# Wider mixer scores, paused scans and another queue for weights in a four-layer convolution stack

## The chip, the cores and the metric

The kernel runs on one core of one Trainium2 chip. The core has five engines that work beside each other, each on a queue of its own: TensorE (PE in the profile) multiplies matrices, VectorE (DVE) and ScalarE (ACT) work elementwise, GpSimd (POOL) too, and SyncE (SP) issues transfers. The metric is the device time of one execution, in microseconds (us); lower is better. The time before is the median of three runs.

## The reference

The input has 8 images of 256 channels and 32 x 32 places (1024 tokens), in float32. Four layers follow one another, each of the form `x = x + layer(group_norm(x))`, where the group norm has 32 groups and no weights:

- Layer 0 is attention over the 1024 tokens with 8 heads of 64, cosine similarities times 10, and an output projection.
- Layers 1 and 2 are 3 x 3 convolutions, 256 to 256 channels.
- Layer 3 is a long block. It has four Mamba branches (a selective scan over the 1024 tokens, 128 channels x 16 states each), gates and short depthwise convolutions, a second attention with 8 heads of 32 (called the mixer attention here) beside a local depthwise convolution, a joint projection, a layer norm with GELU, a norm over the image, a 3 x 3 depthwise convolution, a layer norm and a last projection.

Cut to what matters here:

```python
x = x + L0(gn(x))            # attention: 8 heads of 64
x = x + conv3x3_a(gn(x))
x = x + conv3x3_b(gn(x))
h = gn(x)
xm  = 4 x selective_scan(layernorm(h))
xm2 = mix(h, xm)
att = softmax(q @ k.T / sqrt(32)) @ v        # 8 heads of 32, from xm2
out = concat(depthwise3(xm2), att) @ fc      # then gelu(layernorm), image norm,
x = x + proj(layernorm(depthwise3x3(out)))   # depthwise 3x3, layernorm, proj
```

## The kernel before, in words

Everything stays in float32. A channel tile is 128 partitions x 1024 tokens, two of them to an image; every matmul has 512 columns where it can.

The work of an image falls into three streams, which belong to different images at one time. `front_attention` and `front_convs` are layers 0 to 2 of image b+1. `scan_layers` is the Mamba part of image b. `back_layers`, `back_out` and `back_end` are the rest of image b-1. The loop at the end of `preact_stack` runs over the images; its `dense()` strings together the first and third stream, and `interleave(dense(), scan_layers(imgs[b]), PACE[b])` weaves the scans between them.

The order is written out by hand. Each generator yields a cost, roughly the PE time of what it has just emitted. `interleave` adds up these costs and emits one scan step whenever the sum has passed another `pace` (1.37 in the middle images, 0.9 in the first, 0.74 in the last), so many steps at once if the cost was large. A scan step is a quarter of a scan unit: the two decays on ACT (`da`), the drive and the weighing on POOL (L956 and L981), the two scans on DVE (`hs`), and after every second unit eight matmuls `y<-hs,sel`. `Paced` adds an order between scan instructions and the last dense instruction of the same engine, so that a scan step doesn't come ahead of the dense work that it was written after. A planner then places the instructions on the engines in order of priority; `urgent()` raises the small operations of a norm outside the scans. All compute calls of `tensor`, `vector` and `scalar` have the line L102 in the profile, the line of the helper; they are told apart by their tiles.

Names that the steps below use:

- `chunk` (L156) loads a block of weights into one of five buffers (`wsp`), by a transfer that SyncE issues. A load waits until PE has used the block five loads earlier. 48 such loads are made for an image.
- `attention` is used by both attentions. A unit is one key block of 128 for two heads: two score matmuls into `big`, an exponential `p<-big` on ACT, and two value matmuls `acc<-p,v`. 64 units make an image. Each float32 matmul shows as two PE instructions in the profile.
- The two score matmuls of a unit lie on different rows of the array. In layer 0 a head has 64 rows (`big<-q,k`, 64*128). In the mixer attention a head has 32 rows (`big<-qk,qk`, 32*128), and the two heads i and i+1 of a pair lie on neighbouring strips.
- `mixer_attention` makes v, then the four projections `qk` (two of q, two of k), then runs the four pairs. `back_layers` computes the local convolution (`local`) before it, and starts the next image's group norm (`begin`) at step 58 of it.
- `group_norm` needs a chain: statistics of the finished tile on DVE, a small matmul with `gmat`, a few operations, a second one, then an inverse root by ten or so small DVE operations (`inverse_root`), then two scalings on ACT that write `im<-xt,shift,rs`, the padded images that the convolution reads.
- `front_convs` yields 4 times for the output projection (13.76 of cost), once after the first group norm, 36 times (1.73 each) for the first convolution, once after the second group norm, and 36 times again.
- `back_end` (the end of the image before: layer norm, image norm, sixteen depthwise operations `dw<-xo,vec,dw` on DVE, layer norm, projection) is dropped into `front_convs` by `amid`, at places that are sums of cost:

```python
ENDS = [74, 77, 88, 99, 114]
[0, 13.7, 20] + [23 + 2.7 * k for k in range(16)] + ENDS
```

At the end a flag is computed from the sums of the softmax. Where it is set, a second version of the layers runs; with these inputs it doesn't.

Of the kernel before, what the change touches and what calls it, by code (L numbers as in the profile page):

```python
# [11 lines left out]
F32 = mybir.dt.float32  # L12
I32 = mybir.dt.int32
AF = mybir.ActivationFunctionType
ALU = mybir.AluOpType
# [18 lines left out]
def preact_stack(ctx: ExitStack, tc: tile.TileContext, I, out, cols):  # L34
# [29 lines left out]
    def work(name):  # L64
        return tp.tile([P, TP], F32, tag="t", name=name)
# [4 lines left out]
    def big_tile():  # L70
        return ps_big.tile([P, N], F32, tag="big", name="big")
# [68 lines left out]
    def col(name, i=0, rows=slice(0, P)):  # L140
        at = cols[name] + i
        return vec[rows, at : at + 1]
# [7 lines left out]
    def chunk(name, i):  # L150

        src = fc_w if name == "fcw" else I[name]
        k, n = src.shape[2:]
        t = wsp.tile([P, HALF], F32, tag="w", name="w")
        t = t[:, 0 : k * n].rearrange("p (k n) -> p k n", n=n)
        nc.sync.dma_start(out=t, in_=src[i])  # L156
        return t

    minw = resident("minw")
# [59 lines left out]
    fc_w = wdp.tile([2, P, 4, P], F32, tag="fc_w", name="fc_w")  # L219
    half_d = wp.tile([P, NB], F32, name="half_d")  # L220
    vector.tensor_scalar_mul(half_d, vec[:, cols["mD"] : cols["mD"] + NB], 0.5)
    half_qb = wp.tile([P, 2], F32, name="half_qb")
    vector.tensor_scalar_mul(
        half_qb, vec[:, cols["qpwb"] : cols["qpwb"] + 2], 0.5
# [846 lines left out]
    def mixer_attention(x2, img, exact=False):  # L1071


        v = vp.tile([P, NKT, 8, 64], F32, tag="v", name="v3")
        vector.memset(v[:, :, :, 32:64], 1.0)
        wv = chunk("ainv", 0)
        for kt in range(0, NKT, 4):
            ps = big_tile()
            for i in range(4):
                for c in range(2):  # L1080
                    tensor.matmul(
                        ps[:, i * C : (i + 1) * C],
                        inner(x2[c])[:, (kt + i) * P : (kt + i + 1) * P],
                        wv[:, c],
                        start=c == 0,
                        stop=c == 1,
                    )
            vector.tensor_copy(
                v[:, kt : kt + 4, :, 0:32],
                ps.rearrange("p (k a b) -> p k a b", k=4, b=32),  # L1090
            )
            yield 3.8

        qk = {}
        for t in (0, 2, 1, 3):
            qk[t] = work("qk3")
            w = chunk("ainqk", t)
            ps = big_tile()
            for h in range(2):
                for c in range(2):  # L1100
                    tensor.matmul(
                        ps[:, HALVES[h]],
                        w[:, c],
                        inner(x2[c])[:, HALVES[h]],
                        start=c == 0,
                        stop=c == 1,
                    )
            scale = 32.0**-0.5 if t < 2 else 1.0
            vector.tensor_scalar(
                qk[t][:, 0:N], ps, col("ain_b", t), scale, ALU.add, ALU.mult  # L1110
            )
            yield 3.4

        o = img["o3"] = [work("o3_0"), work("o3_1")]

        def head(i):
            t, rows = i // 4, slice((i % 4) * 32, (i % 4) * 32 + 32)

            def take(half, acc):

                vector.tensor_copy(o[t][rows, half], acc)

            return {
                "q": qk[t][rows, 0:N],
                "k": qk[2 + t][rows, 0:N],
                "v": lambda kt: v[:, kt, i, 0:32],
                "rows": rows,
                "take": take,
            }

        if exact:
            attention_exact(head(i) for i in range(8))
            return

        sums = {}

        def pair(i):
            t = i // 4
            rows = [slice((j % 4) * 32, (j % 4) * 32 + 32) for j in (i, i + 1)]

            def v_of(j):
                return lambda kt: v[:, kt, j]

            def take(h, acc, _):
                if t not in sums:
                    sums[t] = dp.tile([4, N], F32, tag="sums4", name="sums")
                both = half_work("both")
                scalar.copy(both, acc)
                for e in range(2):
                    j, at = (i + e) % 4, e * 64  # L1150
                    nc.sync.dma_start(
                        out=o[t][rows[e], HALVES[h]], in_=both[at : at + 32]
                    )
# [4 lines left out]
                if i % 4 == 2 and h == 1:  # L1158
                    ot = o[t][:, 0:N]

                    return invert(
                        sums[t], 4, 32, lambda r: vector.tensor_mul(ot, ot, r)
                    )

            return {
                "q": [qk[t][r, 0:N] for r in rows],
                "k": [qk[2 + t][r, 0:N] for r in rows],
                "v": [v_of(i), v_of(i + 1)],
                "take": take,
            }  # L1170

        yield from attention([lambda i=i: pair(i) for i in range(0, 8, 2)], False)

    def back_layers(img, exact=False, begin=None):

# [80 lines left out]
        yield from project("fpw", fd, evac_x2)  # L1256


        local = [work("local0"), work("local1")]
        for t in range(2):  # L1260
            depthwise3(local[t][:, 0:N], x2[t], "lc_w", "lc_b", t)
        for n, cost in enumerate(mixer_attention(x2, img, exact)):
            yield cost
            if n == 58 and begin is not None:
                next(begin)
        img["mix"] = xt, local

    def merge_weights():
# [142 lines left out]
    def drain(*streams):  # L1411
        for s in streams:
            for _ in s:
                pass
# [17 lines left out]
    def amid(stream, other, places):  # L1432
# [7 lines left out]
            spent += cost  # L1440
        yield from other

    def slow(stream):

        for cost in stream:
            yield SLOW * cost

    SLOW = 0.35

    ENDS = [74, 77, 88, 99, 114]  # L1450
    PACE = [0.9] + [1.37] * (batch - 2) + [0.74]
    imgs = [{} for _ in range(batch)]
    drain(
# [3 lines left out]
    for b in range(batch):  # L1457

        def dense():
            last = imgs[b - 1] if b > 0 else None  # L1460
            front = None
            if b + 1 < batch:
                front = front_attention(image_of(b + 1), imgs[b + 1])
            if last is None:
                yield from front
                yield from front_convs(imgs[b + 1])
                return
            for n, cost in enumerate(back_layers(last, begin=front)):
                yield cost
                if n == 2 and front is not None:  # L1470
                    next(front)
            if front is None:
                yield from back_out(last)
                yield from back_end(last, out[b - 1])
                return
            yield from islice(front, 4)
            yield next(front)
            yield from back_out(last)
            yield from slow(front)
            yield from amid(  # L1480
                front_convs(imgs[b + 1]),
                back_end(last, out[b - 1]),
                [0, 13.7, 20] + [23 + 2.7 * k for k in range(16)] + ENDS,
            )

        interleave(dense(), scan_layers(imgs[b]), PACE[b])
# [132 lines left out]
```

## Time and profile before

| what | value |
|---|---|
| time | 6742.33 us, median of 3 (6730.57 to 6764.84) |
| span of the profiled execution | 6722.0 us, 52091 instructions |
| PE busy | 5656.0 us (84%) |
| DVE busy | 3779.4 us (56%) |
| ACT busy | 2682.4 us (40%) |
| POOL busy | 2683.7 us (40%) |
| mean granted TensorE clock | 0.868 |
| chain that ended last, by engine | PE 59%, DVE 20%, DMA 6%, issue 6%, ACT 6% |
| SyncE's weight loads (L156) waiting for PE | 1424.4 us in 209 waits, the longest 90.1 us |

How to read it: the first 1018 us hold the fronts of the first two images and the first image's scans. Then come six stretches of about 792 us, in each of which one image ends, one is scanned and one begins; a seventh of 627 us without a front, and a last one of 308 us in which the last image ends alone. A stretch starts with the first matmul of `back_layers`. [...] at 0.5 a matmul takes twice as long, and PE is as busy as at 1.0. "PE busy" must therefore be read together with the clock.

### The profile page before, as it was taken

The page shows a single profiled execution, that of the slowest core. Times are in us where ns is not written, and L with a number is a line of the kernel's source. Part 1 is how long each engine was busy: PE and PEld are TensorE (multiplying, and loading weights), DVE is VectorE, ACT ScalarE, POOL GpSimd, SP SyncE. Part 2 cuts the span into 40 slices and gives each one's busy share as a digit, 9 for nine tenths or more (in the row PEclk, how much of TensorE's full clock was granted, in tenths as well). Part 3 has the DMA queues.
Part 4 walks back from the last instruction along what each step waited for, and adds up shares of the span by engine and source line. Part 5 has one row for each costly group of instructions (what it writes and reads, how often), then busy time and mean ns, then how long its engine had stood idle before and what let it go on. Part 6 is the DMA issues. An engine that isn't in the chain of part 4 may idle for free.

```text
span 6722.0 us, 52091 instructions
## 1 busy us (share of the span) xinstructions
PE 5656.0 (84%) x17318; PEld 1896.2 (28%) x17318; DVE 3779.4 (56%) x4611; ACT 2682.4 (40%) x3225; POOL 2683.7 (40%) x1297
## 2 busy tenths in 40 slices
PE   8886688996989969998789979899799997968586
PEld 2331133222422234222332223222242223411132
DVE  4247855567446674466645674556743667444522
ACT  3223424553245432554236442455324543234332
POOL 0006662634246250643516343362514535166500
PEclk9987898998989979898888989799897997967697
DMA  1022332322224132321223222231213312232200
GB/s 48 26 59 73 86 84 72 93 66 63 72 74 109 42 82 67 91 76 55 68 70 95 76 63 73 64 109 51 78 53 86 95 48 76 73 82 69 83 21 29
DMA packets 216695, 470.80 MB, mean 70 GB/s; under 512 B 60120, under 2 KB 101720, under 8 KB 214368
## 3 DMA queue, kind: packets, MB, share of 16 engines
q1 hardware_dynamic: 216416, 467.38, 25.1%
q8 instruction: 139, 2.28, 0.1%
q14 instruction: 140, 1.15, 0.1%
HBM read 394.31 MB, written 64.49 MB: 68 GB/s over the span
## 4 chain that ended last, share of the span: by engine, by line
PE 59%; DVE 20%; DMA 6%; issue 6%; ACT 6%; POOL 2%; SPq 1%; ACTq 0%; POOLq 0%; DVEq 0%
PE big L102 36%; PE acc L102 14%; PE da L102 5%; DVE hs L102 5%; PE y L102 3%; DVE dw L102 3%; DVE p L102 2%; DVE u L102 2%; DMA dt<-dt_m 1%; DMA dt_m<-dt 1%; POOL hs L956 1%; ACT da L102 1%; ACT p L102 1%; DVE dt L102 1%; DVE t L102 1%
## 5 line engine op out<-in xcount | busy, mean ns | idle before, releaser
L956 POOL TENSOR_TENSOR hs<-du,bc 128x1024 f32<-128x1024 f32 x512 | 1292.3, 2540 | 1613.4 <-DMA dt<-dt_m 1421.9
L981 POOL TENSOR_TENSOR hs<-hs,bc 128x1024 f32<-128x1024 f32 x512 | 1279.6, 2500 | 959.3 <-DVE hs L102 772.1
L102 ACT ACTIVATE p<-big 128x1024 f32<-128x1024 f32 x1024 | 1039.8, 1021 | 941.3 <-PE big L102 921.5
L102 PE MATMUL acc<-p,v 128*64 128x512 f32 x4096 | 1239.8, 672 | 17.1 <-ACT o L102 15.4
L102 PE MATMUL big<-im,w 128*128 128x512 f32 x2304 | 1085.6, 625 | 88.7 <-ACT im L102 78.1
L102 ACT ACTIVATE da<-dt,a_neg 128x512 f32<-128x512 f32 x1024 | 697.1, 688 | 945.7 <-DVE hs L102 787.1
L102 DVE TENSOR_TENSOR_SCAN hs<-da,hs 128x512 f32<-128x512 f32 x512 | 610.2, 1213 | 581.2 <-ACT da L102 367.6
L102 DVE TENSOR_TENSOR_SCAN hs<-da,carry,hs 128x512 f32<-128x512 f32 x512 | 632.1, 1269 | 374.8 <-POOL hs L956 208.1
L102 DVE TENSOR_TENSOR p<-p 128x1024 f32<-128x1024 f32 x448 | 672.0, 1500 | 283.2 <-ACT p L102 169.1
L102 PE MATMUL big<-qk,qk 32*128 32x512 f32 x2048 | 712.3, 736 | 74.6 <-ACT p L102 72.0
L102 PE MATMUL big<-q,k 64*128 64x512 f32 x2048 | 626.7, 663 | 70.4 <-ACT big L102 30.7
L102 PEld LDWEIGHTS big<-im,w 128*128 128x128 f32 x2304 | 443.5, 198 | 725.9 <-issue 613.6
L980 POOL COPY carry<-hs 128x2 f32<-128x2 f32 x256 | 122.3, 478 | 1093.6 <-DVE hs L102 1078.1
L102 PEld LDWEIGHTS acc<-p,v 128*64 128x64 f32 x4096 | 223.3, 143 | 909.3 <-issue 802.4
L102 PE MATMUL y<-hs,sel 128*32 128x512 f32 x2048 | 361.9, 683 | 79.3 <-POOL hs L981 79.3
L102 PEld LDWEIGHTS big<-qk,qk 32*128 32x128 f32 x2048 | 184.0, 207 | 595.1 <-issue 281.4
L102 PE MATMUL da<-xn,w_minw 64*128 64x512 f32 x256 | 171.3, 756 | 213.0 <-DVE hs L102 197.2
L102 PEld LDWEIGHTS big<-q,k 64*128 64x128 f32 x2048 | 172.0, 192 | 498.9 <-issue 264.1
L102 DVE SCALAR_TENSOR_TENSOR dw<-xo,vec,dw 128x961 f32<-128x961 f32 (+1 forms) x128 | 221.8, 1783 | 29.1 <-ACT dw L102 29.1
L102 PE MATMUL big<-xn,w 128*128 128x512 f32 x512 | 230.0, 600 | 1.2 <-DVE v L102 1.2
L102 PE MATMUL big<-o,w 128*128 128x512 f32 x384 | 179.6, 618 | 10.0 <-DVE o L102 10.0
L102 DVE SCALAR_TENSOR_TENSOR xt<-big,vec,xt 128x1024 f32<-128x1024 f32 x48 | 61.5, 1280 | 196.5 <-PE big L102 196.5
(208 smaller groups left out, 4942.2 us busy)
## 6 DMA issues: line engine op xcount, KB each, us to landing
bc<-bc SPq DMA_DIRECT2D x1024, 128.0 KB
dt<-dt_m SPq DMA_DIRECT2D x512, 128.0 KB
du<-du_m SPq DMA_DIRECT2D x512, 128.0 KB
w<-in_wc SPq DMA_DIRECT2D x192, 192.0 KB
rs<-inv SPq DMA_DIRECT2D x64, 256.0 KB
dt_m<-dt SPq DMA_DIRECT2D x64, 256.0 KB
du_m<-a SPq DMA_DIRECT2D x64, 256.0 KB
xt<-in_x SPq DMA_DIRECT2D x8, 1024.0 KB
```

Source lines behind the costliest of these rows:

```text
L102: made = issue(*args, **kwargs)
L956: nc.gpsimd.tensor_mul(u["hs"], u["du"], both_groups(u["bc"][:, 0]))
L980: nc.gpsimd.tensor_copy(carry[:, u["q"], g : g + 2], hs[:, :, HALF - 1])
L981: nc.gpsimd.tensor_mul(hs, hs, both_groups(u["bc"][:, 1]))
```

## The change

Five edits are made at once.

1. **64-row mixer scores.** The k of a projection tile (four heads of 32 rows) is used as it is, 64 rows at a time. q is written twice, once with the rows of the odd heads set to zero (by DVE) and once with those of the even heads (by ACT), through the column pair `alt` of scales. A score matmul then has 64 rows, in which only one head counts. A pair is now heads i and i+2, and the pairs are 0, 1, 4 and 5.
2. **The second q and k inside the mixer.** `q_and_k(1)` is made when its first pair is asked for, eight units ahead of its use, instead of before the mixer.
3. **The local convolution inside the mixer**, at its steps 34 and 40, instead of before it.
4. **Pauses of the scans (`lull`) and other places for the image's end.** In the steps 0 to 3 and 35 to 40 of `front_convs` the cost is held back, so that no scan steps are emitted ahead of the two group norms; it is paid with the step after. `back_end` begins at 14.7 of cost, behind the first group norm, instead of 0, and its last parts stand later.
5. **Weights on ScalarE's queue.** `chunk` issues its transfers from ACT instead of SyncE.

```diff
-        nc.sync.dma_start(out=t, in_=src[i])
+        nc.scalar.dma_start(out=t, in_=src[i])
...
+    alt = wp.tile([P, 2], F32, name="alt")
+    nc.gpsimd.memset(alt, 0.0)
+    for g in range(4):
+        nc.gpsimd.memset(alt[g * 32 : g * 32 + 32, g % 2 : g % 2 + 1], 32.0**-0.5)
+    alt_b = wp.tile([P, 2, 2], F32, name="alt_b")
+    for t in range(2):
+        vector.tensor_scalar_mul(alt_b[:, t], alt, col("ain_b", t))
...
-        for t in (0, 2, 1, 3):
-            qk[t] = work("qk3")
...
+        def q_and_k(t):
+            for at in (t, 2 + t):
+                w = chunk("ainqk", at)
...
+                if at == t:
+                    q = [work("qk3")[:, 0:N] for _ in range(2)]
+                    vector.tensor_scalar(
+                        q[0], ps, col("ain_b", t), alt[:, 0:1], ALU.add, ALU.mult
                     )
-            scale = 32.0**-0.5 if t < 2 else 1.0
-            vector.tensor_scalar(
-                qk[t][:, 0:N], ps, col("ain_b", t), scale, ALU.add, ALU.mult
-            )
-            yield 3.4
+                    scalar.activation(
+                        q[1], ps, AF.Identity, bias=alt_b[:, t, 1:2], scale=alt[:, 1:2]
+                    )
+                else:
+                    k = work("qk3")[:, 0:N]
+                    vector.tensor_scalar_add(k, ps, col("ain_b", at))
+                yield 3.4
+            qk[t] = q, k
+
+        yield from q_and_k(0)
...
+            if t not in qk:
+                drain(q_and_k(t))
+            q, k = qk[t][0][i % 2], qk[t][1]
...
-                "q": [qk[t][r, 0:N] for r in rows],
-                "k": [qk[2 + t][r, 0:N] for r in rows],
-                "v": [v_of(i), v_of(i + 1)],
+                "q": [q[e * 64 : e * 64 + 64] for e in range(2)],
+                "k": [k[e * 64 : e * 64 + 64] for e in range(2)],
+                "v": [v_of(i), v_of(i + 2)],
...
-        yield from attention([lambda i=i: pair(i) for i in range(0, 8, 2)], False)
+        yield from attention([lambda i=i: pair(i) for i in (0, 1, 4, 5)], False)
...
-        local = [work("local0"), work("local1")]
-        for t in range(2):
+        local = []
+
+        def add_local():
+            t = len(local)
+            local.append(work("local"))
             depthwise3(local[t][:, 0:N], x2[t], "lc_w", "lc_b", t)
+
         for n, cost in enumerate(mixer_attention(x2, img, exact)):
             yield cost
-            if n == 58 and begin is not None:
+            if n in (34, 40):
+                add_local()
+            if n == 56 and begin is not None:
                 next(begin)
...
+    def lull(stream, spans):
+
+        owed = 0.0
+        for n, cost in enumerate(stream):
+            if any(a <= n < b for a, b in spans):
+                owed += cost
+                yield 0.0
+            else:
+                yield cost + owed
+                owed = 0.0
...
-    ENDS = [74, 77, 88, 99, 114]
+    LULLS = (0, 4), (35, 41)
+
+
+    ENDS = [14.7, 18, 24] + [27 + 2.5 * k for k in range(16)] + [79, 84, 92, 99, 112]
...
-                front_convs(imgs[b + 1]),
+                lull(front_convs(imgs[b + 1]), LULLS),
                 back_end(last, out[b - 1]),
-                [0, 13.7, 20] + [23 + 2.7 * k for k in range(16)] + ENDS,
+                ENDS,
```

More of the change, by code (lines that the diff above doesn't have):

```diff
@@ L1094, in mixer_attention @@
         qk = {}
-        for t in (0, 2, 1, 3):
-            qk[t] = work("qk3")
[L1097 to L1106, printed above, removed]
-                    )
-            scale = 32.0**-0.5 if t < 2 else 1.0
-            vector.tensor_scalar(
-                qk[t][:, 0:N], ps, col("ain_b", t), scale, ALU.add, ALU.mult
-            )
-            yield 3.4
+        def q_and_k(t):
+            for at in (t, 2 + t):
+                w = chunk("ainqk", at)
+                ps = big_tile()
+                for h in range(2):
+                    for c in range(2):
+                        tensor.matmul(
+                            ps[:, HALVES[h]],
+                            w[:, c],
+                            inner(x2[c])[:, HALVES[h]],
+                            start=c == 0,
+                            stop=c == 1,
+                        )
[3 more added lines that the diff above has]
+                        q[0], ps, col("ain_b", t), alt[:, 0:1], ALU.add, ALU.mult
+                    )
+                    scalar.activation(
+                        q[1], ps, AF.Identity, bias=alt_b[:, t, 1:2], scale=alt[:, 1:2]
+                    )
+                else:
[4 more added lines that the diff above has]
+        yield from q_and_k(0)
         o = img["o3"] = [work("o3_0"), work("o3_1")]
@@ L1121, in take @@
                 vector.tensor_copy(o[t][rows, half], acc)
+            if t not in qk:
+                drain(q_and_k(t))
             return {
-                "q": qk[t][rows, 0:N],
-                "k": qk[2 + t][rows, 0:N],
+                "q": qk[t][0][i % 2][rows],
+                "k": qk[t][1][rows],
                 "v": lambda kt: v[:, kt, i, 0:32],
@@ L1138, in pair @@
             t = i // 4
-            rows = [slice((j % 4) * 32, (j % 4) * 32 + 32) for j in (i, i + 1)]
+            if t not in qk:
+                drain(q_and_k(t))
+            q, k = qk[t][0][i % 2], qk[t][1]
             def v_of(j):
@@ L1149, in take @@
                 for e in range(2):
-                    j, at = (i + e) % 4, e * 64
+                    j, at = i % 4 + 2 * e, e * 64
                     nc.sync.dma_start(
-                        out=o[t][rows[e], HALVES[h]], in_=both[at : at + 32]
+                        out=o[t][j * 32 : j * 32 + 32, HALVES[h]],
+                        in_=both[at : at + 32],
                     )
@@ L1157, in take @@
                     )
-                if i % 4 == 2 and h == 1:
+                if i % 4 == 1 and h == 1:
                     ot = o[t][:, 0:N]
@@ L1263, in back_layers @@
             yield cost
-            if n == 58 and begin is not None:
+            if n in (34, 40):
+                add_local()
+            if n == 56 and begin is not None:
                 next(begin)
+        while len(local) < 2:
+            add_local()
         img["mix"] = xt, local
```

## The prediction

> **What bounds the kernel now.** I read the page's 40 slices first, then the span cut at the stage boundaries of one image, then the granted clock inside the worst stage, and last the time line around the waits.
>
> ```profile
> PE   8886688996989969998789979899799997968586
> PEclk9987898998989979898888989799897997967697
> ```
>
> PE (TensorE) is busy 84% of the span and no other engine over 56%, but the second line is not flat: the granted clock averages 0.868. Lost clock is lost time on the engine that bounds. One typical image (2601.8 to 3397.7 us, 796 us; its neighbours take 791 to 792) in four stages: up to the mixer's attention, mixer attention, the next image's attention, its convolutions; then the mixer attention of the seventh such stretch, beside the last image's scans:
>
> ```profile
> core 0: us, PE busy (x) PEld busy (x) DVE busy (x) ACT busy (x) POOL busy (x), PEclk, DMA share, GB/s
> 2601.80:2679.30 77.50, 69.43 (x203) 34.94 (x201) 58.72 (x96) 33.63 (x35) 0.00 (x0) 0.91 0.19 62
> 2679.30:2893.90 214.60, 190.70 (x623) 43.32 (x622) 98.67 (x96) 116.83 (x143) 133.80 (x69) 0.83 0.34 90
> 2893.90:3129.20 235.30, 216.72 (x754) 62.81 (x752) 163.35 (x183) 117.60 (x145) 82.83 (x38) 0.96 0.24 65
> 3129.20:3397.70 268.50, 214.34 (x593) 91.82 (x592) 151.66 (x198) 66.76 (x82) 118.37 (x54) 0.86 0.25 71
> 5867.00:6247.30 380.30, 292.13 (x747) 58.59 (x748) 176.72 (x152) 161.21 (x204) 244.85 (x124) 0.69 0.33 84
> ```
>
> The clock records hold two values, 1.0 and 0.5, so a stage's half-clock time is 2 x (1 - PEclk) x length: 73 us in the mixer attention, 19 us in the next image's attention, 75 us in the convolutions. In the mixer PE works through most of it; in the convolutions about half of it is PE standing still. Why the mixer stays slow, in four stretches (same columns):
>
> ```profile
> 2685.60:2716.20 30.60, 27.89 (x58) 5.79 (x60) 4.67 (x4) 11.91 (x14) 12.96 (x8) 0.50 0.35 85
> 3115.70:3119.10 3.40, 3.40 (x10) 0.80 (x8) 0.32 (x1) 1.60 (x2) 0.00 (x0) 0.50 0.00 1
> 3119.10:3125.00 5.90, 5.90 (x24) 1.20 (x20) 5.69 (x6) 2.90 (x3) 0.00 (x0) 1.00 0.01 1
> 6480.00:6600.00 120.00, 118.98 (x462) 28.70 (x464) 1.71 (x4) 64.76 (x67) 0.00 (x0) 1.00 0.05 13
> ```
>
> The 32-row mixer attention runs 30 us at half clock with PE busy 91%. The 64-row attention, after a cold start, is at full clock after one full stretch of 3.4 us. The last line is the mixer of the last image, which began at full clock and kept it: 32 rows don't cause the drop, they fail to end it. I cut the whole trace into the 3.41 us steps on which the clock changes and took half-clock steps in which matmuls stream at least 80% of the time: with mixer scores in them 105 of 108 are followed by another half-clock step, with the first attention's scores 3 of 21. The drops themselves follow waits:
>
> ```profile
> 2684.72 1.28 ACT L102 ACT_TABLE_LOAD   x1 [21.44 <-DMA dt<-dt_m]
> 2688.31 2.08 PE L102 MATMUL big<-qk,qk 32*128 32x512 f32 x4 [6.47 <-ACT p L102]
> 3159.04 0.39 PE L102 MATMUL acc<-mv,gmat 128*128 128x4 f32 x2 [3.64 <-DVE mv L102]
> 3162.82 0.58 PE L102 MATMUL acc<-d,gmat 128*128 128x2 f32 x2 [3.39 <-DVE d L102]
> 3182.12 2.92 PE L102 MATMUL big<-im,w 128*128 128x512 f32 x3 [7.62 <-ACT im L102]
> 3243.64 2.07 PE L102 MATMUL da<-xn,w_minw 64*128 64x512 f32 x2 [22.66 <-DVE hs L102]
> 245.43 4.78 PE L102 MATMUL big<-im,w 128*128 128x512 f32 x7 [3.96 <-ACT im L102]
> ```
>
> The first two: ACT holds a scan's exponential for a transfer, and the mixer's exponentials stand behind it. The next three: the first group norm takes from 3154 (last output-projection matmul) to 3182, 28 us; the last line is the same place in the first image, without scans, where it took from 236.3 to 245.4, 9.1 us. Then PE waits 22.66 us for DVE in the first convolution.
>
> [...]
>
> **The change part by part**, per typical image unless said.
>
> *64-row scores.* Four matmuls a unit remain and take 1.06 us at full clock with either row count (start to start of scores and values at 2767.87 and 2991.23), so nothing is saved directly. What changes is the exit from half clock: every score pair now fills all 128 rows. PE records overlap 59 of the 73 us; half of it, 29.5 us, is lost now. The gaps (6.5, 5.9, 2.6, 4.2 us) mostly stay, because PE still waits in order for scan work. I take three or four cold stretches of 7 us, as in the next stage (19 us in two), 17 us of PE work in all, 8.5 lost: 21 us saved. In the sixth of these stretches (5058.6 to 5283.1, clock 0.77, so 103 us cold, 94 with PE) it is 35. In the seventh (last row of the stage table) 236 us are cold, 176 with PE: 88 at most; POOL, busy 245 of 380, becomes the next limit and its waits cool PE again: 75. The last image's is at full clock already: 0. Half the rows of q are zero. If the gate counts values instead of occupied rows, the whole part is worth 0; no run shows it. I take occupied rows.
>
> *Second q and k inside the mixer.* 7 us of PE work (half of the 13.9 us for four projections) moves from before the mixer into it: 0. Two more ACT operations of 1.24 us: hidden, ACT is busy 117 of 215 there.
>
> *Local convolution into the mixer.* Four DVE operations of 1.28 us and two of ACT leave a stage in which PE idles only 8 of 77.5 us: 0.
>
> *Lulls, and the image end behind the first norm.* In the new order no scan stands between the statistics and the shift on DVE, at either group norm. At the first, PE still has 32 small layer-norm matmuls (about 7 us) ahead of the convolution, so not 9 but 13 us: 28 - 13 = 15, I take 14. At the second, 17 us from 3299 to 3316, these matmuls (6.96 us in one row) now stand behind the convolution's first ones: 10 us, 6 saved. The scans held back (13.76 cost, 10 steps, 2.5 scan units of 2 x 1.24 us on DVE, then 7 steps) come at once afterwards. The first convolution takes 117 us (3182 to 3299) with DVE busy 87 and PE 89; in the new order the wait of 22.66 us falls later and with 62 instead of 30 of the convolution's 72 matmuls ahead of it, but DVE's sum grows to about 90. I take 6 us saved. The second convolution gets the layer-norm matmuls and late scans: 5 us lost. Sum 21.
>
> *Weights on ACT.* The wait for fc_w (6.03 us at 2925) goes, since its load now stands in the mixer: 5.5. 48 issues of 0.33 us make 16 us of ACT's sequencer: hidden. Each can also hold ACT until PE frees a buffer; behind it are p and da, for which PE and the scans wait. In the new order each load stands near the matmul that frees its buffer, so I take 0; the other end is below. Two more table loads, 2.6 us: hidden, ACT is busy 67 of 268 there.
>
> Sum: 21 + 21 + 5.5 = 47.5 us in each of five images, 35 + 26.5 = 61.5 in the sixth, 75 in the seventh; first 1018 us and last 308 us: 0. 237.5 + 61.5 + 75 = 374, and 6742 - 374 = **6368, say 6370 us**.
>
> **The rivals.**
> - *The gate counts values, or waits cool PE as often as before.* For it: half of q is zero. Against: the layout of occupied rows alone separates 105 of 108 from 3 of 21. The 215 us of the mixer are missing (5 x 21 + 35 + 75): 6585.
> - *DVE takes back what the lulls give.* For it: DVE is busy 52 of 64 us in the first convolution's first part already. Then the 21 us are missing six times: 6370 + 126 = 6496.
> - *Weight loads hold ACT.* For it: SyncE's 1424 us in 209 waits, 178 us an image. If a third of them delayed PE, 59 us an image would be lost in eight images: 6370 + 472 = 6842, slower.
>
> **How the numbers follow.** Forecast 0.62, gate 0.12, DVE 0.16, ACT slower 0.10. The lower end: POOL no limit in the seventh stretch, one cold stretch of 7 us less and 15 us more from the first convolution in each image, some 150 us: 6220. The upper end takes in the first two rivals and the missing fc_w gain: 6640. Faster 0.86, same 0.04, slower 0.10.
>
> **What would show it.** Right: clock over 0.92 in mixer stages and the seventh under 320 us; 12 to 15 us to the first convolution; no wait on fc_w. Wrong: half-clock stretches of 20 us in the mixer, a PE wait over 20 us for DVE in the first convolution, or ACT idle before p with the releaser a weight buffer.

## The result, and the profile after

The changed kernel takes 6547.26 us (median of 4 runs, 6539.40 to 6553.38) against 6736.45 us of the kernel before on the same chip (4 runs): ratio 0.9719, 95% interval 0.9674 to 0.9763. It is faster by 189 us; 374 had been forecast (6370 us). The time lies in the range, and half of the gain is missing.

The page of the changed kernel, PE and its clock in 40 slices:

```profile
PE   8886788998889979899889988899889998867596
PEclk9997889999999989999999999899889998978697
```

The mean granted clock rose from 0.868 to 0.900; the dips beside the mixers are mostly gone, the drop near the end is not. The clock records hold 1.0 and 0.5 alone and, but for one in each run, last multiples of 3.41 us; at 0.5 a record `big<-im,w` begins 0.85 us after the one before it, at 1.0 0.43 us (medians of either kernel). The stages of the changed kernel that answer to those shown of before (up to the mixer's attention, mixer attention, next image's attention, convolutions with the image end, and the seventh mixer attention). The columns are busy time of each engine with its number of instructions, the granted clock, DMA share and rate:

```profile
core 0: us, PE busy (x) PEld busy (x) DVE busy (x) ACT busy (x) POOL busy (x), PEclk, DMA share, GB/s
2556.50:2628.60 72.10, 62.55 (x187) 31.82 (x185) 52.99 (x91) 33.55 (x35) 0.00 (x0) 0.91 0.18 59
2628.60:2828.30 199.70, 176.67 (x628) 44.05 (x630) 103.42 (x99) 117.57 (x143) 129.91 (x67) 0.91 0.37 97
2828.30:3053.00 224.70, 216.07 (x754) 62.16 (x754) 163.57 (x178) 117.96 (x144) 87.74 (x38) 0.98 0.25 68
3053.00:3321.60 268.60, 224.04 (x601) 90.92 (x602) 164.35 (x205) 71.13 (x86) 121.19 (x56) 0.90 0.26 73
5691.80:6055.10 363.30, 259.86 (x753) 57.18 (x754) 178.83 (x153) 165.98 (x207) 234.80 (x119) 0.79 0.34 87
```

Against the rows of before: 5 us less up to the mixer's attention, 15 less in it (clock 0.83 to 0.91), 11 less in the next image's attention, and **nothing in the convolutions**, 268.5 before and 268.6 after, though the lulls and the late image end were made for that stage. The seventh mixer attention gives 17 us where 75 were forecast. The first stretch, to the first matmul of `back_layers`, grew from 1018.5 to 1028.1 us.

PE's time line at the first group norm of the same image (start, duration, engine, line, operation, number, and in brackets the wait before it and what ended it):

```profile
3075.95 5.40 PE L102 MATMUL big<-o,w 128*128 128x512 f32 x8 [1.99 <-DVE o L102]
3084.28 0.59 PE L102 MATMUL acc<-mv,gmat 128*128 128x4 f32 x2 [2.94 <-DVE mv L102]
3085.52 0.59 PE L102 MATMUL acc<-d,gmat 128*128 128x2 f32 x2 [0.65 <-DVE d L102]
3086.04 1.93 PE L102 MATMUL y<-hs,sel 128*32 128x512 f32 x8
3087.90 6.99 PE L102 MATMUL acc<-mean_w,ln_sq 128*128 128x1 f32 x32
3094.75 2.05 PE L102 MATMUL big<-im,w 128*128 128x512 f32 x2
```

From the end of the projection (3081.3) to the first convolution matmul (3094.7) it is 13.4 us, as forecast, and before it was 27.7. So the norm did become short; the question is where its 14 us went.

### The profile page after: what moved, and what is told of

It reads as the page before. It is cut to its first block, busy times and chain, and to the rows that moved or that the text cites. A ratio compares the mean times of both kernels' runs of the same rounds, so it can differ in the third digit from the quotient of the medians.

```text
span 6540.1 us, 52160 instructions
## 1 busy us (share of the span) xinstructions
PE 5570.3 (85%) x17318; PEld 1876.8 (29%) x17318; DVE 3861.4 (59%) x4613; ACT 2718.7 (42%) x3253; POOL 2701.6 (41%) x1302
## 5 line engine op out<-in xcount | busy, mean ns | idle before, releaser
L989 POOL TENSOR_TENSOR hs<-hs,bc 128x1024 f32<-128x1024 f32 x512 | 1296.2, 2533 | 744.1 <-DVE hs L102 684.6
L102 PE MATMUL acc<-p,v 128*64 128x512 f32 x4096 | 1187.5, 652 | 21.1 <-ACT both L102 12.1
L102 DVE TENSOR_TENSOR p<-p 128x1024 f32<-128x1024 f32 x448 | 718.7, 1604 | 303.9 <-ACT p L102 246.6
L102 PE MATMUL big<-qk,qk 64*128 64x512 f32 x2048 | 685.2, 691 | 113.1 <-ACT p L102 101.3
L102 PE MATMUL y<-hs,sel 128*32 128x512 f32 x2048 | 429.8, 681 | 201.4 <-POOL hs L989 178.9
L102 PEld LDWEIGHTS big<-qk,qk 64*128 64x128 f32 x2048 | 187.6, 198 | 556.1 <-issue 275.0
L102 PEld LDWEIGHTS y<-hs,sel 128*32 128x32 f32 x2048 | 56.3, 113 | 486.8 <-POOL hs L989 298.1
```

Of the source, the lines that this page charges most:

```text
L102: made = issue(*args, **kwargs)
L989: nc.gpsimd.tensor_mul(hs, hs, both_groups(u["bc"][:, 1]))
```

## The experiments

Twelve kernels, each timed against the kernel before. First what the three parts of the change are worth (64-row scores with the moves into the mixer; weights on ScalarE's queue; lulls with the new places of the image end), then what makes the third a loss.

| kernel | us | ratio to before, 95% |
|---|---|---|
| mixer part alone (e1) | 6597.8 | 0.9806 (0.9766 to 0.9847) |
| weights alone (e10) | 6541.6 | 0.9738 (0.9701 to 0.9775) |
| mixer part and weights, no lulls (e5) | 6468.9 | 0.9635 (0.9609 to 0.9661) |
| all three: the change | 6547.3 | 0.9719 (0.9674 to 0.9763) |
| mixer part and lulls (e3) | 6644.3 | 0.9881 (0.9842 to 0.9921) |
| the change with 32-row scores (e2) | 6758.4 | 1.0039 (1.0020 to 1.0057) |

And the stages of one typical image in five of them, cut at the same instructions (us; the third image that ends in the trace):

| stage | before | weights (e10) | mixer (e1) | both (e5) | change |
|---|---|---|---|---|---|
| up to the mixer's attention | 77.4 | 78.7 | 72.1 | 73.7 | 72.1 |
| mixer attention | 214.7 | 214.2 | 199.8 | 203.0 | 199.7 |
| next image's attention | 235.3 | 226.2 | 236.2 | 223.6 | 224.7 |
| rest of attention, projection | 25.2 | 23.7 | 27.6 | 27.5 | 28.4 |
| first group norm | 27.7 | 24.5 | 27.9 | 25.7 | 13.4 |
| first convolution | 116.3 | 100.3 | 116.7 | 101.0 | 113.2 |
| second group norm | 17.1 | 17.4 | 17.8 | 18.3 | 15.8 |
| second convolution | 82.2 | 83.2 | 81.5 | 81.7 | 97.9 |

**e1, the mixer part alone.** Weights back on SyncE, no lulls, old places:

```diff
-        nc.scalar.dma_start(out=t, in_=src[i])
+        nc.sync.dma_start(out=t, in_=src[i])
-                lull(front_convs(imgs[b + 1]), LULLS),
+                front_convs(imgs[b + 1]),
-    ENDS = [14.7, 18, 24] + [27 + 2.5 * k for k in range(16)] + [79, 84, 92, 99, 112]
+    ENDS = [0, 13.7, 20] + [23 + 2.7 * k for k in range(16)] + [74, 77, 88, 99, 114]
```

> The kernel before with the mixer part of the change alone: 64-row scores, second q and k and local convolution inside the mixer; weights on SyncE, convolutions and image end as before. Theory (occupied rows end the half clock): in the two stage tables the mixer attention fell by 17 us in each of five images, 27 in the sixth and 17 in the seventh, 129 us, so about 6605 us with mixer half-clock time of 25 to 45 us an image. Rival (the gain comes from the weights' queue and the convolutions): above 6690 us. Second rival (the mixer part is worth more and the other parts give some of it back): below 6560 us.

Measured: 6597.8 us, 136 less than before, with 37.5 us of half clock in the mixer attention (71.7 before). The theory's number held, though its 129 us was too high a reading: the mixer stages of the change are 9 to 18 us shorter in the five images, 115 us in all. Of 46 dense half-clock windows (matmuls streaming at least 80% of a 3.4 us window) with mixer scores 31 are followed by full clock; before it was 3 of 108. Half of q is zeros here, so no more rows of q hold values than before, and half clock ends all the same: **what counts in these kernels is the rows in use, not the rows of q that hold values**.

**e2, 32-row scores in the changed kernel.** One q again, each head on its own 32 rows:

```diff
-                "q": [q[e * 64 : e * 64 + 64] for e in range(2)],
-                "k": [k[e * 64 : e * 64 + 64] for e in range(2)],
+                "q": [q[r] for r in rows],
+                "k": [k[r] for r in rows],
```

> The changed kernel with 32-row scores again (one q a projection, pairs of heads as in the change, each on its own 32 rows), all else as in the change. Theory (occupied rows): the mixer attention is back to 70 us of half clock an image, and dense half-clock windows with its scores are again followed by half-clock windows in over 9 of 10; 130 us slower, about 6675 us. Rival (moving q, k and the local convolution into the mixer gave it): within 20 us of 6547.

Measured: 6758.4 us, 211 slower, more than expected. The longest typical mixer attention, and that of the last image (columns as above; the profiled execution is the slowest of e2's twenty, 6779 us):

```profile
2685.40:2925.40 240.00, 224.76 (x628) 51.33 (x629) 100.04 (x99) 117.01 (x142) 127.48 (x67) 0.72 0.30 81
...
6486.80:6665.20 178.40, 178.11 (x518) 41.47 (x520) 9.33 (x10) 70.31 (x72) 0.00 (x0) 0.75 0.04 10
```

The same 628 matmul records take 240 us at clock 0.72 instead of 200 at 0.91. The typical mixers are at half clock for 91 to 137 us here, more than the 72 of the kernel before (why more is open), and 186 of 198 dense half-clock windows are followed by another. The last image's mixer, at full clock throughout in the kernel before (130.8 us), now takes 178.4 with 88.7 us of half clock. It begins at full clock, after a short wait for `qk` that the kernel before doesn't have, and the clock drops 2 us later. In the change, and in the ten other kernels with 64 rows, the same stage follows the same wait and the clock doesn't drop. PE in e2:

```profile
6486.82 1.99 PE L102 MATMUL big<-qk,qk 32*128 32x512 f32 x8 [1.38 <-DVE qk L102]
6489.07 2.08 PE L102 MATMUL big<-qk,qk 32*128 32x512 f32 x4 [0.27 <-ACT p L102]
```

And in the change:

```profile
6290.02 1.99 PE L102 MATMUL big<-qk,qk 64*128 64x512 f32 x8 [1.47 <-DVE qk L102]
6292.32 1.13 PE L102 MATMUL big<-qk,qk 64*128 64x512 f32 x4 [0.32 <-ACT p L102]
```

So here the row count decides the drop too (88.7 us of half clock against none), and not only how long half clock lasts; with 32 rows it was seen once.

**e3, weights on SyncE in the changed kernel.** The first two lines of e1's diff alone.

> The changed kernel with the weight loads on SyncE's queue again. In its order on TensorE 54 runs of two sum matmuls y<-hs,sel stand alone, against 124 in the changed kernel, so 35 fewer groups of four are split, at 0.98 us each. Theory: the queue of ScalarE saves the wait on fc_w (6 x 5.5 us) and costs the splits (35 us): within 20 us of 6547. Rival A (weight loads hold ScalarE): faster by 60 us or more. Rival B (the split groups cost nothing): slower by 30 us or more.

Measured: 6644.3 us, 97 slower: the number of rival B, though it doesn't show that split groups cost nothing (e4 asks that). The wait on fc_w was the smaller part of what this queue is worth.

**e10, weights alone.** The kernel before with `nc.scalar.dma_start` in `chunk`, one line.

> The kernel before with the weight loads on ScalarE's queue and nothing else. With 64-row scores and without lulls this edit was worth 129 us (6598 to 6469). Theory (it lets TensorE run on with convolution and projection matmuls whose weights stood behind blocked scan loads, whatever the scores): the stage of the next image's attention falls from 235 to 224 us, the first convolution from 116 to about 101, and the time by 100 to 150 us, to about 6600. Rival (it needs the rest of the change): within 40 us of the kernel before.

Measured: 6541.6 us, 172 less than before: more than the 100 to 150 expected, and not to be told from the whole change. In the stage table it takes 9 us from the next image's attention and **16 from the first convolution**; the mixer's half clock stays at 71.7 us, so it is another cause than e1's. In the seventh mixer it takes 28 (380.3 to 352.5). How, is seen by e1 and e5, which differ in the queue of the weights alone. PE's waits for weights in all of e1 (us in total, times, longest):

```profile
PE big L102 <- DMA w<-in_wqk: 84.2, 6, 14.2
PE big L102 <- DMA w<-in_wc: 7.7, 2, 7.5
```

In e5 no such line is left; the six waits on in_wqk, 14 us each, are the 13 us by which the attention stage fell. In the first convolution it is the order. PE in e1, after the same `y<-hs,sel`:

```profile
3177.73 2.69 PE L102 MATMUL big<-im,w 128*128 128x512 f32 x4
3203.04 2.07 PE L102 MATMUL da<-xn,w_minw 64*128 64x512 f32 x2 [22.62 <-DVE hs L102]
3205.04 6.10 PE L102 MATMUL big<-im,w 128*128 128x512 f32 x8
```

SyncE in the same 30 us of e1 (SPq is its queue; a start after a gap is a wait in order):

```profile
3170.86 6.70 SPq L951 DMA_DIRECT2D bc<-bc  x8
3177.66 0.37 SPq L156 DMA_DIRECT2D w<-in_wc  x1
3194.37 1.70 SPq L951 DMA_DIRECT2D bc<-bc  x4
3196.17 0.84 SPq L156 DMA_DIRECT2D w<-in_wc  x2
```

And PE in e5, 48.7 us earlier:

```profile
3129.02 11.82 PE L102 MATMUL big<-im,w 128*128 128x512 f32 x22
3143.68 3.66 PE L102 MATMUL y<-hs,sel 128*32 128x512 f32 x8 [2.85 <-DVE u L102]
3147.28 3.70 PE L102 MATMUL big<-im,w 128*128 128x512 f32 x8
3154.34 2.07 PE L102 MATMUL da<-xn,w_minw 64*128 64x512 f32 x2 [3.36 <-DVE hs L102]
```

The matmul `da<-xn,w_minw` starts 25.3 us after the first line in either: VectorE works off the same queue in both, image-end taps and then the two scans that free the tile. In e1 four convolution records stand before the matmul that needs those scans, and PE idles 22.62 us; in e5 thirty convolution records and a group of sums stand there, and it idles 2.85 us before the sums and 3.36 after. The weights were also late in e1. The block that leaves SyncE at 3177.66 needs the buffer of the block five before, which PE was done with at 3149, 28 us earlier; in e5 the same block follows its buffer by 3 us. The one after it left only at 3196, behind a scan load that was held for a buffer. So in this stretch the weights were not in the scans' way; the scans' loads were in the weights' way, and PE's planned order had fewer convolution matmuls in front. The transfers themselves are no faster from ACT's queue: from the issue of an in_wc load to the end of its last packet it is 2.10 us in the kernel before and 2.07 in e10 (medians). That the planner chose this order because of the queue was not tried by itself, so how much of the 172 us is late weights and how much is order stays open.

**e5, without the lulls.** The last two edits of e1's diff in the changed kernel.

> The changed kernel without the lulls and with the image end at the places of the kernel before. Theory (what the first group norm gains, the second convolution gives back): the first group norm is back at 26 to 28 us and the second convolution at 82 us, the convolution stage 268 us as with the lulls, and the time within 20 us of 6547. Rival A (the prediction: 21 us an image): slower by about 126 us. Rival B (the lulls cost more than they bring): faster by 25 us or more.

Measured: 6468.9 us, 78 less than the change, or 57 by the ratios, since the kernel before was 23 us faster on e5's chip (the ratio is lower by 0.0084; the intervals don't meet). Rival B: the lulls cost. The first norm back to 25.7 us, first convolution, second norm, second convolution of e5:

```profile
3059.60:3085.40 25.80, 12.14 (x50) 8.36 (x49) 18.41 (x44) 10.73 (x13) 10.67 (x5) 0.61 0.13 33
3085.40:3186.30 100.90, 89.36 (x225) 33.40 (x226) 80.72 (x76) 32.09 (x40) 67.01 (x32) 0.90 0.35 94
3186.30:3204.70 18.40, 13.01 (x54) 9.12 (x52) 14.18 (x42) 4.04 (x5) 4.66 (x2) 0.73 0.38 102
3204.70:3286.40 81.70, 81.70 (x217) 34.14 (x218) 29.88 (x30) 15.42 (x20) 30.36 (x13) 0.98 0.20 62
```

The same four of the change:

```profile
3081.30:3094.70 13.40, 9.81 (x45) 8.01 (x45) 9.73 (x22) 1.75 (x2) 4.65 (x2) 0.59 0.06 15
3094.70:3208.00 113.30, 94.88 (x231) 33.77 (x231) 92.48 (x95) 42.16 (x51) 67.11 (x31) 0.91 0.27 74
3208.00:3223.70 15.70, 3.04 (x12) 1.20 (x12) 12.45 (x24) 2.63 (x4) 11.03 (x7) 0.57 0.69 172
3223.70:3321.60 97.90, 94.21 (x265) 39.72 (x266) 36.51 (x51) 19.67 (x25) 34.95 (x15) 0.98 0.20 61
```

Look at the last row of each: PE is busy in nearly all of both, so the second convolution was full, and what moves into it makes it longer. From 217 to 265 records: 32 layer-norm sums (3.6 us), eight broadcasts of the mean (3.5) and eight more sums `y<-hs,sel` (4.9 us more) came in. The second norm of the change has 12 PE records where e5 has 54: the work that filled the wait is gone, and the wait is nearly as long, because VectorE's statistics end it. Over the whole stage of 254.3 us against 268.6, with PE's time at half clock counted half: 8.2 us more PE work (of it 7.7 in the sums `y`, which had been issued in fours and now come in pairs), 9.7 us more idle time, and 3.6 us less lost to half clock. **The norms got shorter by 15 us, and the convolutions longer by 28.**

**e9, lulls with the old image end; e12, the first lull alone with the new one.**

```diff
-    ENDS = [14.7, 18, 24] + [27 + 2.5 * k for k in range(16)] + [79, 84, 92, 99, 112]
+    ENDS = [0, 13.7, 20] + [23 + 2.7 * k for k in range(16)] + [74, 77, 88, 99, 114]
```

```diff
-    LULLS = (0, 4), (35, 41)
+    LULLS = ((0, 4),)
```

> The changed kernel with its lulls, but with the image end at the places of the kernel before. Theory (holding scans back costs, as they come back beside the second convolution): the first group norm stays at 14 us, the second convolution at 95 us or more, and the time within 20 us of 6547. Rival (the later image end costs, not the lulls): the second convolution is back at 82 us and the time at 6490 us or less.

> The changed kernel with the lull at the first group norm alone; the image end stays at the places of the change. Theory (the first lull saves as much at the norm as it costs in the first convolution, and the second one makes the loss): the first norm stays at 14 us and the first convolution at 113, the second convolution falls from 100 us to 85 or less, and the time to 6480 us or less. Rival A (each held-back scan costs, wherever): the second convolution at 90 to 96 us, about 6510 us. Rival B (the later image end makes the second convolution long): it stays at 98 us or more, within 20 us of 6547.

Measured: 6581.7 us (0.9805, 0.9766 to 0.9844) and 6558.0 us (0.9735, 0.9691 to 0.9779). In e9 the first norm stays at 13.4 and the second convolution at 103 us, as the theory had it, but the time is 35 us above 6547 and not within 20. In e12 the second lull is gone, but the second convolution stays at 102.5: rival B's numbers, and my guess that the second lull made the loss falls. Nor did the second lull shorten its norm: without it the second norm is 10.3 to 10.7 us, the size forecast for the lull, and the first convolution takes 118 us instead of 113.

The two runs don't separate the lulls from the later image end. `amid` counts the same costs that `lull` holds back, so in e9 the parts at 74 and 77, which were written just before and just behind the second norm, come after the second convolution's first matmuls. That convolution has as many records in e9 as in the change:

```profile
3241.00:3343.90 102.90, 95.74 (x265) 40.01 (x266) 38.21 (x51) 19.55 (x25) 34.96 (x15) 0.97 0.19 60
```

Among them are the same 32 sums and eight broadcasts, so the image end is late in all three kernels. Whether it would cost without any lull was not run.

**e4 and e8, sums tied together.** In the change many groups of four sum matmuls are split in two. On PE's time line (two records a matmul, so the eight `y<-hs,sel` after every second unit are four matmuls):

```profile
3131.67 1.06 PE L102 MATMUL y<-hs,sel 128*32 128x512 f32 x8
3132.66 8.86 PE L102 MATMUL big<-im,w 128*128 128x512 f32 x20
3141.45 1.05 PE L102 MATMUL y<-hs,sel 128*32 128x512 f32 x4
3142.43 1.13 PE L102 MATMUL big<-im,w 128*128 128x512 f32 x2
```

From its start to the next matmul's a whole group of eight records takes 0.99 us, and half a group 0.98. The edit, in the changed kernel (e4) and in e5 (e8):

```diff
-            for u in pair:
+            for u in reversed(pair):
...
+                    last = made
...
+                    if last is not None:
+                        tc.add_manual_dep(
+                            made.ins,
+                            last.ins.name,
...
```

> The changed kernel with the four sum matmuls of two scan units tied together on TensorE in order (those of the second unit first), so that 251 of 256 groups stand whole, against 185 before. Theory (a group of four in a row takes 0.99 us, split in two it takes 2 x 0.98): some 62 groups made whole, 60 us faster, about 6487 us, and y<-hs,sel busy falls from 430 us to below 340. Rival (the halves run in time that TensorE has to spare, or waiting for the second half costs as much): within 20 us of 6547.

> The changed kernel with the tied sum matmuls and without the lulls: a candidate for the fastest. If both edits act by themselves: 17 us below the kernel without lulls. Rival (tying the sums only moves the wait): equal to it within 15 us.

Measured: 6529.9 us (0.9711, 0.9672 to 0.9751) and 6461.7 us (0.9624, 0.9597 to 0.9650), neither to be told from its parent. The groups of the sums in the pages of the change and of e4:

```profile
L102 PE MATMUL y<-hs,sel 128*32 128x512 f32 x2048 | 429.8, 681 | 201.4 <-POOL hs L989 178.9
```

```profile
L102 PE MATMUL y<-hs,sel 128*32 128x512 f32 x2048 | 316.1, 687 | 236.3 <-POOL hs L989 236.2
```

PE's work fell by 114 us and the time by 17, inside the uncertainty: 35 us came back as waits before the sums alone, and the idle time of the convolution stage rose from 41 to 45 us to 49 to 53. The stage takes 266 to 270 us, as in the change (265 to 272), so PE's work alone doesn't set its length; in the whole kernel nearly all of PE's waits before the sums (236.2 of 236.3 us) end with a product of GpSimd. The split sums are therefore not what makes the change's convolutions long.

**e6, without taps; e7, without weighing.** e6 leaves out 14 of the 16 shifted multiply-adds of the image end on VectorE, e7 the multiplication of the scan's result by C on GpSimd; neither computes the whole function.

```diff
+                if n > 0:
+                    yield 0.5
+                    continue
```

```diff
-            nc.gpsimd.tensor_mul(hs, hs, both_groups(u["bc"][:, 1]))
```

> The changed kernel with 14 of the 16 shifted multiply-adds of the image end's depthwise convolution left out (they are VectorE operations of 1.26 to 3.3 us); the order on TensorE is the same. Two image ends stand at the end of the program on the path by themselves: 2 x 14 x 1.26 = 35 us are saved in any case. Theory (VectorE's scans and taps set the pace of the convolution stage): the stage falls from 268 us to below 245 and the time to 6370 us or less. Rival (TensorE's own work of 204 us and the chain of the norms set it): the stage stays at 258 us or more, 6450 to 6512 us.

> The changed kernel without GpSimd's multiplication of the scan's result by C (one of its two operations of 2.35 us or more for each of 64 units an image). Theory (the chain of scans over GpSimd sets the seventh mixer): the seventh mixer attention falls from 363 us to below 320. Rival (VectorE's scans and ScalarE set it): 345 us or more there. If the convolution stage too waits for GpSimd, it falls from 268 us to below 255.

Measured: 6455.7 and 6130.8 us. Without the taps the stage falls to 260 or 261 us in five images and 255 in the sixth (first convolution 103 to 104, second 102 in most images): the rival's numbers, in the time too, but with 8 to 10 us gone from the first convolution. Without the weighing the stage falls to 243 to 246, the typical mixer to 182 to 185, the next image's attention to 214, and the time by 417 us (393 by the ratios), more than with any other edit. So the convolution stage does wait for GpSimd, by its results or by VectorE's operations that are long beside its products (an image-end tap of 128x961 takes 1.2 us by itself in the change, and up to 3.3 beside them); the two were not told apart. The seventh mixer of e7:

```profile
5323.30:5656.40 333.10, 252.58 (x757) 57.24 (x758) 179.97 (x154) 166.03 (x207) 125.02 (x72) 0.84 0.37 96
```

333 us, which is neither theory's number: the weighing is worth 30 us there, and at 333 us PE still stands idle for 80 of them. The scans limit this stage, but not by GpSimd alone.

**e11, the last pace** (0.74 to 0.9, in e5).

> The changed kernel without lulls and with the last pace at 0.9 instead of 0.74, so that fewer scan steps go beside the seventh mixer attention and more beside what follows. Theory (the seventh mixer waits for scans): the mixer attention there falls from 361 us to 340 or less, and of that a part is left in the sum of the stretch (610 us before): 5 to 20 us faster than 6469. Rival (the scans that are left over run alone afterwards): the same or slower.

Measured: 6452.9 us (0.9601, 0.9564 to 0.9639), not to be told from e5 by the intervals, though all four times, on another chip, lie below all four of e5. The seventh mixer fell from 361 to 285 us and its stretch from 610 to 555, but the scans that were left made the last stretch 353 instead of 307 us. It has the lowest time of the full computations; e5, e8 and e11 are all faster than both kernels.

## Why the prediction was half right

*64-row scores: right in kind, too high in size.* Forecast 21 us an image, 35 in the sixth, 75 in the seventh, 215 in all. Alone (e1) the mixers gave 14 in a typical image (213.8 to 199.8), 25 in the sixth, 25 in the seventh, and the part as a whole 136. The term that was mis-sized is PE's work at half clock that is left: 17 us were assumed, and 28 to 33 measured (59 before), of which half is lost; (59 - 31) / 2 is the 14 us. The waits stayed, 20 to 22 us of idle PE in a mixer against 23 before, and the clock goes on dropping at them: in the change it falls five or six times in each of the first six mixers, each time after a 3.41 us step in which PE stood idle for 1.6 us or more. The 1.06 us given for the four matmuls of a unit are its two score matmuls (four records) alone; a whole unit takes 2.07 us at full clock in the kernel before, with either row count, and 3.91 at half. In the seventh the assumption that GpSimd would only become a limit near 305 us failed: PE is idle for 103 of 355 us in e1, against 88 of 380 before, so the waits took back part of the gain. The clock over 0.92 that I had named as a sign was 0.91. That 32 rows don't cause the drop doesn't hold for the last image of e2. The rival "the gate counts values", by which half clock would have lasted as before, is refuted by e1 (31 of 46 dense windows followed by full clock) and e2 (12 of 198), as far as values of q go.

*Second q and k, local convolution inside the mixer: 0, roughly right.* The stage before the mixer fell by 4 to 5 us with e1, and the last image's mixer rose from 130.8 to 136.7.

*Weights on ACT: far too low.* I took 5.5 us an image, the wait on fc_w, 33 in all. The queue is worth 129 us after e1 (115 by the ratios), 97 in the changed kernel (e3; 109 by the ratios) and 172 alone. The step that was wrong is to cost the edit by the waits of PE that named a weight. The issues themselves are 48 x 0.33 = 16 us an image on either engine; what e1 and e5 show is loads that no longer stand behind held transfers, and another order on PE. The bigger part, 16 us in the first convolution, was the 22.66 us before `da<-xn,w_minw`, whose releaser is a scan; I had read it as a matter of the lulls. The rival "weight loads hold ACT" forecast a slower kernel and got a faster one, though waits of its kind appear: in the change ACT waits 151.6 us in 14 waits for PE's `big` before `da`.

*Lulls and image end: the step that failed.* Forecast 21 us saved an image, 126 in all. e5 against the change: the stage is 14 us longer with them in the image shown (9 to 17 in the others), 57 to 78 us in all. Term by term, from e5 to the change: first norm -14 forecast, -12.3 measured; second norm -6 and -2.5; first convolution -6 and **+12**; second convolution +5 and **+16**. The norms' terms took the wait as empty time. The second norm's wait held 32 sums and most of the broadcasts, and these had to go somewhere: PE in the second convolution was already busy all the time. The first norm kept its 32 sums; the scan work that left it came back in the first convolution, where PE's waits for GpSimd's products before the sums `y` grew from 4.2 to 13.2 us. The second norm failed for another reason too. I took its layer-norm sums as what delayed it; they left, and this remained, VectorE in the change:

```profile
3210.67 1.26 DVE L102 SCALAR_TENSOR_TENSOR xt<-big,vec,xt 128x1024 f32<-128x1024 f32 x1
...
3211.84 1.21 DVE L102 TENSOR_TENSOR_SCAN hs<-da,hs 128x512 f32<-128x512 f32 x1
...
3212.98 1.26 DVE L102 BATCH_NORM_STATS2 st<-xt 128x6 f32<-128x512 f32 x2
...
3215.36 1.56 DVE L102 TENSOR_TENSOR d<-mv,g 128x2 f32<-128x2 f32 x1
...
3216.95 2.26 DVE L102 TENSOR_TENSOR d<-d 128x2 f32<-128x2 f32 x1
```

A scan still stands ahead of the statistics, and two tiny operations, 0.16 us each by themselves, take 3.8 us beside GpSimd's products. The rival "DVE takes back what the lulls give" (6496) had the right stage, but VectorE's taps are not the whole cause: without 14 of 16 (e6) the first convolution is 8 to 10 us shorter and the second still 102 us. Nor are the split sums (e4). The bookkeeping is shown, where the work went and which stages grew; which engine's work makes the two convolutions 28 us longer was not isolated, nor the pauses of the scans from the later image end.

*The sum.* Mixer and weights were forecast at 248 us, and e5 is 244 below the kernel before on its chip (6468.86 against 6713.27): two errors that met, which is luck. What is missing from the sum is what the lulls were to bring and what they cost.

## What to carry to other kernels

Before closing a wait, see whether it is empty: list what the waiting engine does in it, and where that work would go; if the next stage is full, as here, moving it there can cost more than it saves. Cost a queue by what stands behind its blocked head in both directions, and by the order it makes the planner write, and not only by waits that name its transfers. When parts of a change are bundled, time each alone and each taken out; here one line alone gave nearly as much as all, and the bundle without one of its parts gave more. Check, too, what else an edit moves: the lulls moved the image end as well.

## What the runs showed of the hardware

- Mixer scores on 32 rows a head, two heads at a time, kept the half clock in 105 of 108 (before) and 186 of 198 (e2) windows of 3.4 us in which PE streams for at least 80%; the layout that fills the rows, half of q zeros, did in 16 of 52 in the change. After the same wait of 1.4 us at full clock the last image ran 88.7 us at half clock with 32 rows and none with 64.
- Four 128x32 matmuls on four column groups take as long together (0.99 us at full clock) as two of them (0.98), if the other two come later. Tying them together took 114 us off their busy time, but no time that can be told from noise.
- VectorE's 128x2 operations, 0.16 us by themselves, took up to 2.3 us beside GpSimd's 128x1024 products, and its 128x961 multiply-adds up to 3.3 instead of 1.2. In the second norm shown above two of them took 1.56 and 2.26 us beside products of 2.34 us each. So the length of a norm's chain of tiny operations hangs here on what GpSimd happens to do; by what mechanism was not shown.
